# A fused graph-and-convolution layer on one core: when the convolution's sums are evacuated, when position factors are made, and in which order a batch's graph pieces are issued

## The chip, the core and the metric

The kernel runs on one core of a Trainium2 chip. The metric is the device time of one execution in microseconds (us), and smaller is better. In the profile TensorE is called PE (its weight loads PEld), VectorE DVE, ScalarE ACT, GpSimd POOL; SP is the engine whose queue issues all DMAs here.

## The reference

The layer takes x, 32 batches of 512 rows with 256 columns, and a 512x512 adjacency mask for each batch, all in float32. With h the normalised and rectified x:

```python
h = jnp.maximum(_layernorm(x, axis=-1), 0.0)
x = x + _L0_gnn_ref(h, adj, ...)

# inside _L0_gnn_ref (its x is h above, d = 256)
xc = jnp.transpose(x, (0, 2, 1))
h = relu(_bn(_conv1d(xc, conv1_w, 0), ...))          # width 1
h = _bn(_conv1d(h, conv2_w, 8), ...)                 # width 17
x_conv = jnp.transpose(relu(h + xc), (0, 2, 1))
s = x @ w_se.T + b_se                                # 3 position values a row
sq = jnp.sum(s * s, axis=-1)
dist = sq[:, :, None] + sq[:, None, :] - 2.0 * jnp.einsum('bnd,bmd->bnm', s, s)
A = jnp.exp(-dist) * mask
msg = relu(x @ w_msg.T + b_msg)
x_nmp = jnp.einsum('bnm,bmd->bnd', A, msg)
x_in = jnp.concatenate([x_conv, x_nmp], axis=-1)
gi, gh = x_in @ w_ih.T + b_ih, x @ w_hh.T + b_hh
r = sigmoid(gi_r + gh_r); z = sigmoid(gi_z + gh_z)
nn_ = jnp.tanh(gi_n + r * gh_n)
return (1.0 - z) * nn_ + z * x
```

## The kernel before

**Two streams of work.** The 32 batches are taken in 8 rounds of G = 4. The convolution of width 17 is computed by a nested fast scheme: from the rows of a round, VectorE forms 25 operand sets (`operands`, `fives`: five first-level operands `x1`, and five `x2` from each), 25 transformed weight sets `w` are loaded again for each round, and 25 products of matmuls go to the PSUM tile `ps_c` (3 buffers). `convolution` issues each product in two halves. `summed(g)` takes the 25 products, in five groups of five, and adds them into the tile `y`: a product is copied or added out of PSUM at once (`n`, `z`, `s`), while the later additions are put into the list `SUMS` and issued one by one by `sum_some`, at every second half of a product. At the second product of a group whatever still stands in `SUMS` is issued. When a round's 25 products are done, the rest of `SUMS` is issued at once, and then eight ScalarE evacuations (L393, two for each of the four batches) write `y` with scale and shift into the four `xconv` tiles.

The other stream is `others(g)`. In round g it runs `rest` for the four batches of the round before, and, ahead of the fourth, `rows(g+1)`: the transposes and the width-1 convolution for the next round. The normalisation of those rows (`norm`) is cut into pieces of DVE and POOL work that `norm_some` issues, one with each step of the others, once `rows_begin` has loaded x; that is at the third batch (n == 2).

**The order.** Nothing is planned at run time: each engine's instructions run in the order in which this program issues them. `step_conv` and `step_other` advance the two streams, and the variable `ahead` holds their balance: each step of the others says its TensorE time in us (the number that it yields), which is multiplied by a share (81/214 in most rounds) and paid for by half products of 1.65. Behind the last round the four last batches run without any convolution.

**One batch, `rest(b, following)`.** In order: load of the mask and of the hidden rows `hTb` if they are not loaded yet; `positions(b)` (one PE piece, two DVE instructions that write rows of `left` and `right`, two ACT squares that write others: L462 to L465); the residual addition of the convolution and its relu (L527, L528); `messages` twice (PE, then DVE and ACT); `kernel_exp` for four columns of the 512x512 kernel matrix (L480 matmul of `left` and `right`, L481 exponential); `finish` of the batch before in two pieces (L500 transposes of its result `o_sb`, L504 addition, store); `masked` for four columns (L488 transposes of the mask, L489 multiplication into `at`). That is called the graph part here. Then the loads for the following batch are issued, and the gates follow: for each half o the hidden part of the candidate, at o = 0 the two `gather` matmul groups, the reset gate r, the update gate z, the candidate n, and on POOL the last three operations, which write `o_sb`. PSUM tiles: `ps_acc` has 3 buffers (messages, exponentials, gathers, gates), `ps_tr` has 2 (positions, masks, finishes, row transposes).

Of the kernel before, what the change touches and what calls it, by code (L numbers as in the profile page):

```python
# [29 lines left out]
G = 4  # L30
U = 57
# [9 lines left out]
def kernel(  # L41
# [293 lines left out]
    def sum_some(pieces=1):  # L335
        while SUMS and pieces:
            SUMS.pop(0)()
            pieces -= 1

    def summed(g):  # L340


        y = cv.tile([P, 3, 3, NZ], F32, name="y")
        yf = y.rearrange("p f e n -> p f (e n)")

        def add(dst, a, b, op=ALU.add):
            SUMS.append(lambda: nc.vector.tensor_tensor(dst, a, b, op=op))  # L347

        def copy(dst, src, scale):
            SUMS.append(lambda: nc.scalar.activation(dst, src, AF.Copy, scale=scale))  # L350

        def twice(dst, a, b):
            SUMS.append(
                lambda: nc.vector.scalar_tensor_tensor(dst, a, 2.0, b, op0=ALU.mult, op1=ALU.add)
            )

        for j1 in ORDER:
            ps = yield
            n3 = cv.tile([P, NZ], F32, name="n", bufs=3)
            nc.scalar.activation(n3, ps, AF.Copy)  # L360
            ps = yield
            sum_some(len(SUMS))
            z = y[:, 0] if j1 == 3 else cv.tile([P, 3, NZ], F32, name="z")
            ends = z[:, 0:3:2, :]
            zf = z.rearrange("p e n -> p (e n)")
            nc.vector.tensor_tensor(z[:, 0, :], ps, n3, op=ALU.add)  # L366
            ps = yield
            nc.vector.scalar_tensor_tensor(z[:, 2, :], n3, 4.0, ps, op0=ALU.mult, op1=ALU.add)
            ps = yield
            n2 = cv.tile([P, NZ], F32, name="n", bufs=3)  # L370
            nc.scalar.activation(n2, ps, AF.Copy)
            ps = yield
            s = cv.tile([P, NZ], F32, name="s")
            nc.vector.tensor_tensor(s, ps, n2, op=ALU.add)
            nc.vector.tensor_tensor(n2, ps, n2, op=ALU.subtract)
            add(ends, ends, s[:, None, :].to_broadcast([P, 2, NZ]))
            twice(z[:, 1, :], n3, n2)
            if j1 == 3:
                copy(yf[:, 1], zf, 2.0)
                copy(yf[:, 2], zf, 4.0)  # L380
            elif j1 in (0, 4):
                add(yf[:, j1 // 2], yf[:, j1 // 2], zf)
            else:
                for e in range(3):
                    add(yf[:, e], yf[:, e], zf, ALU.subtract if (e, j1) == (1, 2) else ALU.add)
        sum_some(len(SUMS))
        if late is None:
            late_pools()
        for b in range(g * G, (g + 1) * G):
            xc = XC[b] = late.tile([P, ND, 9 * U], F32, name="xconv", bufs=4)  # L390
            for o in range(ND):
                c = o * NU + b % G * U
                nc.scalar.activation(  # L393
                    xc[:, o, :].rearrange("p (u e f) -> p f e u", e=3, f=3), y[:, :, :, c : c + U],
                    AF.Identity, bias=bn2_sh[:, o : o + 1], scale=bn2_sc[:, o : o + 1],
                )
        yield

    AHEAD, AHEAD_W = 4, 2
    XC = {}  # L400

    def convolution():

# [110 lines left out]
    def rest(b, following):  # L514

        if b not in MS:
            load_adj(b)
        if b not in HB:
            load_h(b)
        msg = late.tile([P, NT, D], F32, name="msg")  # L520
        at = late.tile([P, NT, N], F32, name="at")
        xnmp = late.tile([P, ND, N], F32, name="xnmp")
        positions(b)
        yield 1.75
        xc = XC.pop(b)
        xconv = xc[:, :, :N]
        nc.vector.tensor_tensor(xconv, xconv, HB[b], op=ALU.add)  # L527
        nc.scalar.activation(xconv, xconv, AF.Relu)  # L528
        for c in range(0, NT, 2):
            messages(b, msg, c)  # L530
            yield 1.8
        for c in range(NT):
            kernel_exp(at, c)
            yield 0.87
        while waiting:
            for c in range(0, NT, 2):
                finish(*waiting[0], c)
                yield 0.55
            waiting.pop(0)
        for c in range(NT):  # L540
            masked(b, at, c)
            yield 0.55
        MS.pop(b)
        if following is not None:
            load_adj(following)
            load_h(following)
        hT = HB.pop(b)
        o_sb = late.tile([P, ND, N], F32, name="o_sb")
        x_in = [xconv[:, i, :] for i in range(ND)] + [xnmp[:, i, :] for i in range(ND)]

        def cols(o, g):
            return slice(g * D + o * P, g * D + (o + 1) * P)

        def hidden(o, g):
            return [(whh[:, i, cols(o, g)], hT[:, i, :]) for i in range(ND)]

        def given(o, g):
            return [(wih[:, i, cols(o, g)], x_in[i]) for i in range(2 * ND)]

        for o in range(ND):  # L560
            ps_h = acc.tile([P, N], F32, name="ps_acc")
# [15 lines left out]
            yield 5.2  # L577
            ps_z = acc.tile([P, N], F32, name="ps_acc")
            matmul_sum(ps_z, hidden(o, 1) + given(o, 1))
            z = late.tile([P, N], F32, name="z")  # L580
            nc.scalar.activation(z, ps_z, AF.Sigmoid, bias=brz[:, ND + o : ND + o + 1])  # L581
            yield 5.2
            ps_n = acc.tile([P, N], F32, name="ps_acc")
            matmul_sum(ps_n, given(o, 2))
            nc.vector.tensor_tensor(r, ps_n, r, op=ALU.add)  # L585
            nc.scalar.activation(  # L586
                r, r, AF.Tanh,
                bias=vec[:, _COL["b_ih"] + 2 * ND + o : _COL["b_ih"] + 2 * ND + o + 1],
            )

            t = late.tile([P, N], F32, name="gate_t")
            nc.gpsimd.tensor_tensor(t, hT[:, o, :], r, op=ALU.subtract)  # L592
            nc.gpsimd.tensor_tensor(t, z, t, op=ALU.mult)
            nc.gpsimd.tensor_tensor(o_sb[:, o, :], r, t, op=ALU.add)
            if o == ND - 1:
                load_res(b)
            yield 3.46
        waiting.append((b, o_sb))

    def rows_begin(g):  # L600
# [34 lines left out]
    def others(g):  # L635


        bs = list(range((g - 1) * G, g * G)) if g > 0 else []
        for n, b in enumerate(bs[:-1]):
            if n == 2 and g + 1 < NG:  # L640
                rows_begin(g + 1)
            yield from rest(b, b + 1)
        if not bs:
            rows_begin(g + 1)
        yield "rows wanted", g + 1
        if g + 1 < NG:
            yield from rows(g + 1)
        yield "rows made", g + 1
        for b in bs[-1:]:
            yield from rest(b, b + 1)  # L650
# [3 lines left out]
    for g in range(NG):  # L654
        other = others(g)
        share = 81.0 / (214.0 if 0 < g < NG - 1 else 196.0 if g else 18.0)
        ahead = 0.0
        end = ended = False
        blocked = False

        def step_other():

            nonlocal ahead, end, made
            if end:
                return False
            norm_some()
            got = next(other, None)
            if got is None:
                end = True
                return False  # L670
            if isinstance(got, tuple):
                if got[0] == "rows wanted":
                    while freed < g:
                        step_conv()
                else:
                    made = got[1]
                return True
            ahead += got * share
            return True
# [78 lines left out]
```

## Time and profile before

| | |
|---|---|
| time, median of 3 runs | 2671.2 us (2666.92 to 2671.62) |
| the profiled execution | 2667.14 us |
| its span, first to last instruction | 2665.4 us |
| mean granted TensorE clock | 0.949 of full speed |
| PE busy | 2441.9 us |
| DVE busy | 1228.8 us |
| ACT busy | 640.5 us |
| POOL busy | 328.6 us |
| DMA | 231.15 MB, 87 GB/s on average |

All durations in this document's rows come from that profiled execution. A row of instructions reads: start, duration, engine, line of the kernel, operation, output <- inputs, shape, count, and in brackets the idle time of the engine just before with what ended it. A row of waits reads: engine, tile and line that waited, what it waited for, us in total, times, longest. A matmul in float32 is counted twice (two passes each).

### The profile page before, as it was taken

The page shows a single profiled execution, that of the slowest core. Times are in us where ns is not written, and L with a number is a line of the kernel's source. Part 1 is how long each engine was busy: PE and PEld are TensorE (multiplying, and loading weights), DVE is VectorE, ACT ScalarE, POOL GpSimd, SP SyncE. Part 2 cuts the span into 40 slices and gives each one's busy share as a digit, 9 for nine tenths or more (in the row PEclk, how much of TensorE's full clock was granted, in tenths as well). Part 3 has the DMA queues.
Part 4 walks back from the last instruction along what each step waited for, and adds up shares of the span by engine and source line. Part 5 has one row for each costly group of instructions (what it writes and reads, how often), then busy time and mean ns, then how long its engine had stood idle before and what let it go on. Part 6 is the DMA issues. An engine that isn't in the chain of part 4 may idle for free.

```text
span 2665.4 us, 20881 instructions
## 1 busy us (share of the span) xinstructions
PE 2441.9 (92%) x8192; PEld 1505.2 (56%) x8192; DVE 1228.8 (46%) x1766; ACT 640.5 (24%) x882; POOL 328.6 (12%) x240
## 2 busy tenths in 40 slices
PE   6689999899997999979999799997999979997998
PEld 4566556465564565645556465664556646664444
DVE  7983364534545344444444445344454444443222
ACT  3232213212133121222212222222212132212222
POOL 1000121110101111011110011100111101111111
PEclk9789999999998999989999899998999989998999
DMA  5242223123231232322232122221232212220110
GB/s 214 100 170 72 79 95 127 47 79 103 79 119 47 71 111 81 117 71 65 92 105 102 55 87 101 97 79 63 87 103 93 82 64 86 87 95 25 54 40 24
DMA packets 108996, 231.15 MB, mean 87 GB/s; under 512 B 8418, under 2 KB 57698, under 8 KB 108258
## 3 DMA queue, kind: packets, MB, share of 16 engines
q1 hardware_dynamic: 108898, 229.82, 25.1%
q8 instruction: 64, 1.05, 0.2%
q14 instruction: 34, 0.28, 0.0%
HBM read 183.13 MB, written 46.66 MB: 86 GB/s over the span
## 4 chain that ended last, share of the span: by engine, by line
PE 80%; DVE 12%; ACT 4%; issue 2%; DMA 1%; POOL 1%; SPq 0%; POOLq 0%; DVEq 0%; ACTq 0%
PE ps_acc L86 51%; PE ps_c L86 20%; PE ps_acc L480 4%; ACT xconv L393 2%; PE ps_tr L488 2%; DVE x L239 2%; PE ps_tr L86 2%; DVE y L347 1%; PE ps_tr L217 1%; DVE x L242 1%; PE ps_tr L500 1%; DVE at L489 1%; DVE st L182 1%; DVE y L504 1%; DVE z L347 1%
## 5 line engine op out<-in xcount | busy, mean ns | idle before, releaser
L86 PEld LDWEIGHTS ps_c<-x,w 128*128 128x128 f32 x3200 | 619.8, 195 | 180.0 <-issue 153.0
L86 PE MATMUL ps_c<-x,w 128*128 128x228 f32 x3200 | 694.1, 364 | 22.7 <-DVE z L366 10.7
L86 PE MATMUL ps_acc<-hTb,whh 128*128 128x512 f32 x768 | 365.1, 601 | 0.0
L86 PE MATMUL ps_acc<-xconv,wih 128*128 128x512 f32 x768 | 360.8, 592 | 0.0
L86 PE MATMUL ps_acc<-xnmp,wih 128*128 128x512 f32 x768 | 360.6, 592 | 0.0
L592 POOL TENSOR_TENSOR gate_t<-hTb,r 128x512 f32<-128x512 f32 x64 | 91.1, 1423 | 2020.3 <-issue 1272.9
L480 PE MATMUL ps_acc<-right,left 67*128 67x512 f32 x256 | 155.3, 739 | 120.8 <-ACT left L465 99.2
L573 DVE SCALAR_TENSOR_TENSOR r<-ps_acc,vec,r 128x512 f32<-128x512 f32 x64 | 48.1, 751 | 441.9 <-ACT r L571 441.9
L86 PEld LDWEIGHTS ps_acc<-xnmp,wih 128*128 128x128 f32 x768 | 145.3, 189 | 184.2 <-issue 184.2
L86 PEld LDWEIGHTS ps_acc<-xconv,wih 128*128 128x128 f32 x768 | 145.8, 190 | 157.3 <-issue 156.9
L86 PE MATMUL ps_acc<-at,msg 128*128 128x512 f32 x512 | 228.5, 592 | 0.0
L585 DVE TENSOR_TENSOR r<-ps_acc,r 128x512 f32<-128x512 f32 x64 | 44.3, 692 | 396.8 <-PE ps_acc L86 396.8
L86 PEld LDWEIGHTS ps_acc<-hTb,whh 128*128 128x128 f32 x768 | 146.0, 194 | 117.0 <-issue 116.1
L571 ACT ACT_TABLE_LOAD x32 | 41.1, 1283 | 652.1 <-PE ps_acc L86 652.1
L242 DVE SCALAR_TENSOR_TENSOR x<-x,x 128x471 f32<-128x471 f32 (+1 forms) x184 | 159.4, 866 | 5.2
L480 PEld LDWEIGHTS ps_acc<-right,left 67*128 67x128 f32 x256 | 54.5, 225 | 185.6 <-ACT left L465 102.5
L239 DVE TENSOR_TENSOR x<-x 128x471 f32<-128x471 f32 x200 | 158.0, 808 | 1.4
L86 PEld LDWEIGHTS ps_acc<-at,msg 128*128 128x128 f32 x512 | 97.2, 190 | 106.4 <-issue 106.2
L494 DVE COPY xnmp<-ps_acc 128x512 f32<-128x512 f32 x64 | 44.3, 692 | 236.4 <-PE ps_acc L86 236.4
L581 ACT ACTIVATE z<-ps_acc,brz 128x512 f32<-128x512 f32 x64 | 44.0, 688 | 341.2 <-PE ps_acc L86 341.2
L586 ACT ACTIVATE r<-r,vec 128x512 f32<-128x512 f32 x64 | 46.2, 722 | 307.5 <-DVE r L585 307.5
L86 PE MATMUL ps_acc<-hT,w 128*128 128x512 f32 x256 | 119.1, 607 | 0.0
(90 smaller groups left out, 2242.0 us busy)
## 6 DMA issues: line engine op xcount, KB each, us to landing
w<-wd SPq DMA_DIRECT2D x175, 512.0 KB, 3.3
m_sb<-in_adj_dram SPq DMA_DIRECT2D x32, 1024.0 KB, 5.3
x_sb<-in_x_dram SPq DMA_DIRECT2D x32, 512.0 KB, 6.2
hd<-hT SPq DMA_DIRECT2D x32, 512.0 KB, 2.9
hTb<-hd SPq DMA_DIRECT2D x32, 512.0 KB, 6.2
y<-in_x_dram SPq DMA_DIRECT2D x64, 256.0 KB, 4.0
out_dram<-y SPq DMA_DIRECT2D x64, 256.0 KB, 2.2
wd<-w SPq DMA_DIRECT2D x25, 512.0 KB, 2.6
```

The lines of the kernel that those rows point to most:

```text
L86: nc.tensor.matmul(ps, lhsT, rhs, start=(i == 0), stop=(i == len(pairs) - 1))
L239: nc.vector.tensor_tensor(dst, get(a), get(b), op=ALU.subtract)
L242: nc.vector.scalar_tensor_tensor(dst, a, -2.0, b, op0=ALU.mult, op1=ALU.add)
L347: SUMS.append(lambda: nc.vector.tensor_tensor(dst, a, b, op=op))
L393: nc.scalar.activation(xc[:, o, :].rearrange("p (u e f) -> p f e u", e=3, f=3), y[:, :, :, c : c + U], AF.Identity, bias=bn2_sh[:, o : o + ...
L480: nc.tensor.matmul(ps, left[:, c * P : (c + 1) * P], right, start=True, stop=True)
L488: nc.tensor.transpose(ps[:, n * P : (n + 1) * P], m[:, n, c * P : (c + 1) * P], ident)
L494: nc.vector.tensor_copy(xnmp[:, d, :], ps)
L573: nc.vector.scalar_tensor_tensor(r, ps_h, vec[:, _COL["b_hh"] + 2 * ND + o : _COL["b_hh"] + 2 * ND + o + 1], r, op0=ALU.add, op1=ALU.mult,)
L585: nc.vector.tensor_tensor(r, ps_n, r, op=ALU.add)
L586: nc.scalar.activation(r, r, AF.Tanh, bias=vec[:, _COL["b_ih"] + 2 * ND + o : _COL["b_ih"] + 2 * ND + o + 1],)
L592: nc.gpsimd.tensor_tensor(t, hT[:, o, :], r, op=ALU.subtract)
```

## The change

Five things are moved; the arithmetic stays.

1. The eight evacuations are no longer issued at the round's end. Each is an entry of `SUMS`, behind the last additions, so that it is issued during the next round's first steps. `step_other` now issues one entry of `SUMS` at each step while more than four are left. The tile `y` is taken only when the next round first writes it. A batch that needs its `xconv` issues entries until its own evacuations are out.
2. `positions` of the following batch is called between the two halves of the gates. Only a batch whose mask was not loaded ahead (the first) still calls it at its start.
3. The graph part alternates: messages ahead of columns 0 and 2, and for each column the exponential and at once its mask; behind columns 1 and 3 one piece of `finish`.
4. The residual addition and relu move behind the graph part.
5. `rows_begin` is called at the first batch of a round (n == 0) instead of the third, and, except in round 0, `norm_some` at every second step only.

```diff
     def summed(g):
-        y = cv.tile([P, 3, 3, NZ], F32, name="y")
-        yf = y.rearrange("p f e n -> p f (e n)")
+        y = yf = None
...
             ps = yield
             sum_some(len(SUMS))
+            if y is None:
+                y = cv.tile([P, 3, 3, NZ], F32, name="y")
+                yf = y.rearrange("p f e n -> p f (e n)")
             z = y[:, 0] if j1 == 3 else cv.tile([P, 3, NZ], F32, name="z")
...
-        sum_some(len(SUMS))
         if late is None:
             late_pools()
         for b in range(g * G, (g + 1) * G):
-            xc = XC[b] = late.tile([P, ND, 9 * U], F32, name="xconv", bufs=4)
             for o in range(ND):
-                c = o * NU + b % G * U
-                nc.scalar.activation(xc[...], y[:, :, :, c : c + U], AF.Identity, ...)
+                SUMS.append(lambda b=b, o=o: evacuate(y, b, o))
         yield
+    def evacuate(y, b, o):
+        if o == 0:
+            XC[b] = late.tile([P, ND, 9 * U], F32, name="xconv", bufs=4)
+        c = o * NU + b % G * U
+        nc.scalar.activation(XC[b][...], y[:, :, :, c : c + U], AF.Identity, ...)
+        if o == ND - 1:
+            evacuated.add(b)
...
     def rest(b, following):
         if b not in MS:
             load_adj(b)
-        if b not in HB:
             load_h(b)
+            positions(b)
+            yield 1.75
         msg, at, xnmp = ...
-        positions(b)
-        yield 1.75
-        xc = XC.pop(b)
-        xconv = xc[:, :, :N]
-        nc.vector.tensor_tensor(xconv, xconv, HB[b], op=ALU.add)
-        nc.scalar.activation(xconv, xconv, AF.Relu)
-        for c in range(0, NT, 2):
-            messages(b, msg, c)
-            yield 1.8
         for c in range(NT):
+            if c % 2 == 0:
+                messages(b, msg, c)
+                yield 1.8
             kernel_exp(at, c)
             yield 0.87
-        while waiting:
-            for c in range(0, NT, 2):
-                finish(*waiting[0], c)
-                yield 0.55
-            waiting.pop(0)
-        for c in range(NT):
             masked(b, at, c)
             yield 0.55
+            if waiting and c % 2:
+                finish(*waiting[0], c - 1)
+                yield 0.55
+        waiting.clear()
         MS.pop(b)
         if following is not None:
             load_adj(following)
             load_h(following)
         hT = HB.pop(b)
+        while b not in evacuated:
+            sum_some()
+        xc = XC.pop(b)
+        xconv = xc[:, :, :N]
+        nc.vector.tensor_tensor(xconv, xconv, hT, op=ALU.add)
+        nc.scalar.activation(xconv, xconv, AF.Relu)
...
             yield 3.46
+            if o == 0 and following is not None:
+                positions(following)
+                yield 1.75
         waiting.append((b, o_sb))
...
     def others(g):
-            if n == 2 and g + 1 < NG:
+            if n == 0 and g + 1 < NG:
                 rows_begin(g + 1)
...
         def step_other():
-            norm_some()
+            steps += 1
+            if g == 0 or steps % 2:
+                norm_some()
+            if len(SUMS) > 4:
+                sum_some()
             got = next(other, None)
```

More of the change, by code (lines that the diff above doesn't have):

```diff
@@ L389, in summed @@
         for b in range(g * G, (g + 1) * G):
-            xc = XC[b] = late.tile([P, ND, 9 * U], F32, name="xconv", bufs=4)
             for o in range(ND):
-                c = o * NU + b % G * U
[L393 to L396, printed above, removed]
-        yield
+                SUMS.append(lambda b=b, o=o: evacuate(y, b, o))
+        yield
+    def evacuate(y, b, o):
+        if o == 0:
+            XC[b] = late.tile([P, ND, 9 * U], F32, name="xconv", bufs=4)
+        c = o * NU + b % G * U
+        nc.scalar.activation(
+            XC[b][:, o, :].rearrange("p (u e f) -> p f e u", e=3, f=3), y[:, :, :, c : c + U],
+            AF.Identity, bias=bn2_sh[:, o : o + 1], scale=bn2_sc[:, o : o + 1],
+        )
+        if o == ND - 1:
+            evacuated.add(b)
     AHEAD, AHEAD_W = 4, 2
-    XC = {}
+    XC, evacuated = {}, set()
     def convolution():
@@ L657 @@
         ahead = 0.0
+        steps = 0
         end = ended = False
@@ L661, in step_other @@
         def step_other():
-            nonlocal ahead, end, made
+            nonlocal ahead, end, made, steps
             if end:
                 return False
-            norm_some()
+            steps += 1
[3 more added lines that the diff above has]
+                sum_some()
             got = next(other, None)
```

## The prediction

> **What bounds the kernel now.** I read the page's first lines, then who TensorE waits for, then the granted clock in short stretches, then the order of instructions where the waits are.
>
> ```profile
> span 2665.4 us, 20881 instructions
> PE 2441.9 (92%) x8192; PEld 1505.2 (56%) x8192; DVE 1228.8 (46%) x1766; ACT 640.5 (24%) x882; POOL 328.6 (12%) x240
> ```
>
> TensorE (PE) is busy 92% of the span; VectorE (DVE) and ScalarE (ACT) are not half busy. So only two things can move the time: the 224 us in which PE idles, and stretches in which PE is busy but slow. The waits of PE alone:
>
> ```profile
> PE ps_acc L480 <- ACT left L465: 99.2, 9, 16.0
> ...
> PE ps_tr L488 <- DVE y L504: 17.9, 19, 1.8
> PE ps_acc L480 <- ACT at L481: 15.8, 15, 1.4
> ```
>
> The first row is 44% of the idle time in nine waits. By windows of one round it is one wait of 13.0 us at the start of each of rounds 2 to 7, one of 16.0 us behind the last round, and 5 us elsewhere. The clock by windows of PE (columns: stretch, length, PE busy, granted clock as a share of full speed, DMA): first the start of one round, then three graph parts of that round (its batches 1, 2 and 3), then the whole round.
>
> ```profile
> 1478.00:1518.00 40.00, 26.63 (x90) 0.74 0.13 42
> 1487.00:1499.70 12.70, 0.00 (x0) 0.65 0.14 41
> 1499.70:1510.00 10.30, 10.29 (x18) 0.50 0.00 0
> ...
> 1570.00:1590.00 20.00, 17.88 (x71) 0.91 0.25 83
> 1645.00:1662.00 17.00, 12.68 (x45) 0.80 0.18 55
> 1738.00:1754.00 16.00, 15.58 (x75) 1.00 0.22 69
> ...
> 1493.00:1817.00 324.00, 303.80 (x1024) 0.95 0.25 86
> ```
>
> The round's start loses twice: 13.4 us of idle PE, and then 10.3 us at clock 0.50, which is 5.2 us of lost work: 18.6 us. Batch 1 loses 2.1 idle and at most (1-0.91)x20 = 1.8 of clock; batch 2, with the normalisation's pieces on DVE, 4.3 and at most 3.4; batch 3 only 0.4. The Trainium skill (TensorE: Matmul & The Clock Gate, "What's actually happening") says that PE falls to half rate after an idle window of about 3.4 us and is back after a busy one as long. The fall agrees (0.65 over 12.7 us is half clock from some 4 us into the wait); the return doesn't: 0.50 holds for over 10 us. By the Trainium skill's figure the slow stretch would cost an estimated 1.7 us, not 5.2.
>
> Why the start waits, in order of time (start, duration, engine, line, operation, out<-in, count):
>
> ```profile
> 1478.25 1.88 PE L86 MATMUL ps_tr<-hTb,wse 128*67 128x512 f32 x4
> 1478.45 0.69 DVE L585 TENSOR_TENSOR r<-ps_acc,r 128x512 f32<-128x512 f32 x1 [8.03 <-PE ps_acc L86]
> 1480.27 2.01 DVE L347 TENSOR_TENSOR z<-z,s 128x912 f32<-128x912 f32 x1
> 1482.20 1.69 DVE L354 SCALAR_TENSOR_TENSOR z<-n 128x456 f32<-128x456 f32 x1
> 1483.92 5.52 DVE L347 TENSOR_TENSOR y<-y,z 128x1368 f32<-128x1368 f32 x3
> 1489.48 8.79 ACT L393 ACTIVATE xconv<-y,bn_shift,bn_scale 128x513 f32<-128x513 f32 x8 [9.58 <-DVE y L347]
> 1493.02 1.28 DVE L475 TENSOR_TENSOR msg<-ps_acc,bmsg 128x512 f32<-128x512 f32 x2
> 1494.21 2.08 DVE L239 TENSOR_TENSOR x<-h 128x1415 f32<-128x1415 f32 x1
> 1496.33 1.63 DVE L242 SCALAR_TENSOR_TENSOR x<-x,x 128x1415 f32<-128x1415 f32 x1
> 1498.00 0.79 DVE L239 TENSOR_TENSOR x<-x 128x471 f32<-128x471 f32 x1
> 1498.97 0.68 ACT L465 ACTIVATE left<-ps_tr,bse 3x512 f32<-3x512 f32 x1
> 1499.71 7.20 PE L480 MATMUL ps_acc<-right,left 67*128 67x512 f32 x8 [13.04 <-ACT left L465]
> 1512.35 2.96 DVE L489 TENSOR_TENSOR at<-ps_tr,at 128x512 f32<-128x512 f32 x4
> 1516.07 1.70 PE L86 MATMUL ps_c<-x,w 128*128 128x228 f32 x8
> 1517.61 7.03 PE L86 MATMUL ps_acc<-at,msg 128*128 128x512 f32 x16
> ```
>
> The positions' matmuls are done at 1480. Their factors stand on DVE behind the last sums (until 1489.4) and on ACT behind all eight evacuations (8.79 us, 1.1 each), so the exponential's matmul (L480) starts at 1499.7.
>
> **The change, part by part.** Counts stay: 64 evacuations, 32 positions, the same table loads and DMAs. Only places move.
>
> *Positions one batch ahead.* Two DVE and two ACT instructions of 0.7 us and one PE piece (1.72 us, from 1478.25 to the next start) go between the two halves of the gates, where PE runs without a wait; cost 0. It needs the next batch's hidden rows by then: that load is issued where it was, ahead of the gates. If it came late PE would wait; the only such wait today is the first batch's, which stays in line as it is.
>
> *Evacuations and last sums spread.* One of 13 pieces is now issued with each step of the others and each half product. I worked out the order: last-round tail, z add, z twice, messages 0, half product, y add three times with column 0 and 1 and two statistics pieces between them, evacuations among the columns, finish 0, messages 2, columns 2 and 3. Prices of what PE does there, at full clock, from batch 3 of this round, and of the normalisation's pieces:
>
> ```profile
> 1739.04 3.62 PE L86 MATMUL ps_acc<-wmsg,hTb 128*128 128x256 f32 x16
> ...
> 1744.90 2.74 PE L480 MATMUL ps_acc<-right,left 67*128 67x512 f32 x6
> ...
> 1749.89 1.03 PE L488 MATMUL ps_tr<-ident,m_sb 128*128 128x128 f32 x8
> ...
> L182 DVE BATCH_NORM_STATS2 st<-x_sb 128x6 f32<-128x256 f32 x128 | 51.7, 404 | 18.8 <-DMA x_sb<-in_x_dram 18.8
> L190 DVE TENSOR_SCALAR x_sb<-x_sb,mv,rstd 128x256 f32<-128x256 f32 x128 | 45.2, 408 | 26.2 <-POOL rstd L143 26.2
> L183 DVE BATCH_NORM_AGGREGATE mv<-st 128x2 f32<-128x6 f32 x128 | 23.3, 182 | 4.4
> ```
>
> From the end of the old batch's last gate (time 0, 1478.25 above), DVE in its new order: 0.2 + 1.8 (three ops, 1478.45 to 1480.27) + 1.9 + 1.7 (z) + 0.6 (message) + 0.8 (operand) + 5.5 (y) + one statistics piece 2x(0.40+0.18) = 1.2 + 0.7 (mask of column 0) = 14.4. PE gets there sooner: messages 1.8, half products 2x1.6, two exponentials 2x0.9, two masks 2x0.5: 7.8. Then *finish 0* wants one of the two ps_tr buffers and waits for column 0's multiply: 6.6 us. That is what is late next, and it is long enough to take the clock to 0.50. From 14.4: finish 1.0 and messages 3.6 at half clock (19.0), add 0.7, relu 0.6, exponential 0.6 plus its matmul (21.6), multiply (22.3); then DVE holds a first-level operand, 2.08+1.63+0.79 = 4.5, and a scaling piece 0.8 in front of column 3's multiply: 28.3. The gathering matmul starts there. Today it starts 1517.61-1478.25 = 39.4 after time 0, which includes 1.72 of positions and one half product (1.54) that now comes behind it, so 36.1 of like work. **Gain 7.8 a round start; six of them, 47 us.** Ends: DVE alone (25 us of work up to column 3, less some 2 us that the two z ops lose while POOL runs) could let it start at 23 to 24, a gain of 12; every link waiting for the next could bring 34, a gain of 2. I take the worked value, nearer the rows. The y tile's first write of the new round now waits for the last evacuations; three ps_c buffers cover it.
>
> *Rows begun at batch 0, every other step.* The normalisation leaves batch 2 (loss 7.7) and goes half to the round's start (counted above), half to batch 1 (loss 3.9). I take 3 each for both afterwards: (7.7-3)+(3.9-3) = 5.6 for each of the six rounds that have such rows, **33 us**; ends 0 and 9. Its three x loads go to SP's queue at the round's start: 512 KB each behind weight loads that wait for buffers, and DMA share there is 0.13, so 0; if late, DVE waits with statistics, not the weights.
>
> *Behind the last round.* No convolution is left, so sums are issued only after the graph part. Rows (the old round's last batch, then the batch after):
>
> ```profile
> 2426.82 1.88 PE L86 MATMUL ps_tr<-hTb,wse 128*67 128x512 f32 x4
> ...
> 2469.09 1.88 PE L86 MATMUL ps_acc<-hTb,whh 128*128 128x512 f32 x4
> ...
> 2498.27 1.88 PE L86 MATMUL ps_tr<-hTb,wse 128*67 128x512 f32 x4
> ...
> 2503.94 1.27 POOL L594 TENSOR_TENSOR o_sb<-r,gate_t 128x512 f32<-128x512 f32 x1
> ...
> 2513.12 1.88 PE L86 MATMUL ps_acc<-hTb,whh 128*128 128x512 f32 x4
> ```
>
> Today 42.3 us from positions to the reset gate. Afterwards: graph part 12.5 and finish's add 0.8; then DVE: z twice and y adds 0.9+5.5, two evacuations 2.5 on ACT, residual add 1.2, and behind it the copy of the first gather, whose buffer the reset gate needs: 24.1, where PE is ready at about 21. With the positions' 1.72: 25.8. **Gain 16 us**; ends 10 and 20.
>
> *Alternation in the tail.* A batch's graph part takes 2513.12-2498.27 = 14.9 (13.1 without positions) there. New: finish 0 comes 4.5 us after the gates, but POOL writes o_sb until 6.9: PE waits 2.4, and the mask of column 2 waits for its exponential; some 12.5 to 13.5. Taken as 0 to 0.4 worse for three batches: **-1 us**.
>
> The start of the first round keeps its 9.9 us wait for the first load: 0, at most 5 won. **Sum:** 47+33+16-1 = 95 at the worked values; since the half clock behind the new 6.6 us wait will last past the gather's start in some rounds (10 us is what it lasts above), I take off 1 us for each of six: 89. The profiled execution took 2667.1 us (span 2665.4), 4 below the median of 2671.2: 2667-89 = **2578**, which is 93 below the median.
>
> **The rivals.**
>
> *The waits vanish.* If POOL doesn't slow DVE and no wait reaches the length that halves the clock, a start gains 12, both graph parts all but lose their loss (9 a round), the tail 20: 6x12+6x9+18 = 144; with half of the second, 2667-130 = **2537**. For it: batch 3 above, with little else on DVE, runs at clock 1.00. Against: 25 us of DVE work in front of a multiply that PE wants much earlier. The Trainium skill (TensorE: Matmul & The Clock Gate, "Part 4: PE-mode transpose") says transposes do not count as PE work for the clock; alternated with real matmuls they would leave fewer such windows. Rows agree in part: at 0.80 stands the part with the most stalled transposes, but batch 3 has as many at 1.00.
>
> *The wait only changes its name.* Column multiplies queue behind sums and statistics, ACT's exponentials behind evacuations; the start's gather comes at 34, a gain of 2, and batch 1 loses what batch 2 wins (half of 33): 12+16+15 = 43: **2624**. For it: DVE order is strict in the trace, and the change puts 2 to 3 us of statistics where DVE is fullest. Against: the left factors leave the chain altogether, and ACT's 8.8 us block is broken up.
>
> *Slower.* Alternating chains PE exponential, ACT, DVE multiply and the next transpose. If the buffers did not let columns overlap, a column costs 0.9+0.6+0.7 and the hand-overs 0.6 = 2.8, four of them 11, messages 3.5 and finish 1: 15.7 against the tail's 13.1, and batch 1's 1.8 of clock on top: +4.4 for 32 batches = 141, against the 89: **2719**. It decides from 2.8 a batch on. Against: three ps_acc and two ps_tr buffers, and half products between the steps.
>
> **How the numbers follow.** Forecast (2555 to 2600) 0.58; waits vanish 0.20; name changed 0.17; slower 0.05. 2578 is the forecast's. The range 2530 to 2622 takes in the first rival's value and nearly the second's, and leaves out some 0.2; the likeliest case's own is 2555 to 2600. About 0.2% (5 us) is what a measurement of this kernel can tell from no change. Faster 0.93 (the first three cases, less a little), same 0.02, slower 0.05.
>
> **What would show it.** Right: no wait of L480 for left but the first batch's; at each round's start a PE wait of 4 to 8 us before finish (L500) for DVE's multiply, some 31 us from the last gate to the gather by like counting; batch 2's window at clock above 0.9; the time from the last round's end to the reset gate 16 us shorter; POOL named before L500 in the tail. Wrong: waits of L488 and L500 for DVE that sum to over 80 us; clock 0.50 in every graph part; DVE waiting for x loads at the round's start; the gates' positions waiting for hTb.

## The result, and the profile after

The changed kernel takes 2542.9 us (median of 4 runs, 2541.4 to 2544.9). Before, in the same comparison, it is 2669.3 us. The ratio is 0.953, with a 95% interval of 0.951 to 0.954. The profiled execution took 2544.2 us (before 2667.1), so 123 us are to be found between the two traces; the prediction's sum found 89 of them. One execution of all those told of here stands apart: the last experiment's kernel took 6954.8 us once, in the execution that was profiled, and 2488.8 to 2492.6 us in its other four, so nothing is read from its trace.

The first lines of the page after, and the waits of PE alone:

```profile
span 2542.4 us, 20857 instructions
PE 2386.9 (94%) x8192; PEld 1484.4 (58%) x8192; DVE 1224.5 (48%) x1766; ACT 646.4 (25%) x882; POOL 335.2 (13%) x240
```

```profile
PE ps_tr L508 <- DVE at L497: 70.1, 23, 6.2
...
PE ps_tr L86 <- DMA hTb<-hd: 15.5, 1, 15.5
```

The 99.2 us for `left` are gone. In their place stands the wait that the prediction named: finish (L508 now) for the multiplies of the mask (L497), 70.1 us. PE's busy time fell as well, by 55 us for the same 8192 matmuls. The clock explains most of that: laid over the stretches of half clock in the two traces, PE was busy at half speed for 174 us before and 89 us after, which is some 43 us less lost to it, about a third of the 123 us. The other 12 us of the fall I have not placed. Windows of PE as before: the start of a round (time zero, the end of the old batch's last gate, is at 1421.64), its wait, the 4.6 us behind the wait, then the graph parts of batches 1, 2 and 3.

```profile
1418.00:1458.00 40.00, 33.76 (x123) 0.91 0.28 92
1429.00:1435.40 6.40, 0.21 (x2) 0.79 0.00 0
1435.40:1440.00 4.60, 4.54 (x13) 0.55 0.32 81
1497.00:1517.00 20.00, 16.99 (x74) 0.91 0.12 41
1569.00:1586.00 17.00, 16.34 (x76) 1.00 0.17 57
1661.00:1677.00 16.00, 15.97 (x78) 1.00 0.14 49
```

Rows of that start in order of time:

```profile
1421.64 1.89 PE L86 MATMUL ps_acc<-wmsg,hTb 128*128 128x256 f32 x8
...
1423.65 1.10 DVE L346 TENSOR_TENSOR z<-z,s 128x912 f32<-128x912 f32 x1
1423.72 2.16 POOL L599 TENSOR_TENSOR gate_t<-hTb,r 128x512 f32<-128x512 f32 x1 [19.29 <-ACT r L593]
...
1428.04 4.12 DVE L346 TENSOR_TENSOR y<-y,z 128x1368 f32<-128x1368 f32 x2
1428.95 0.60 ACT L489 ACTIVATE at<-ps_acc 128x512 f32<-128x512 f32 x1
...
1433.16 1.55 DVE L346 TENSOR_TENSOR y<-y,z 128x1368 f32<-128x1368 f32 x1
1434.62 0.68 DVE L497 TENSOR_TENSOR at<-ps_tr,at 128x512 f32<-128x512 f32 x1
...
1435.46 1.08 PE L508 MATMUL ps_tr<-ident,o_sb 128*128 128x128 f32 x4 [6.25 <-DVE at L497]
...
1436.34 3.49 PE L86 MATMUL ps_acc<-wmsg,hTb 128*128 128x256 f32 x8
...
1439.67 1.02 PE L488 MATMUL ps_acc<-right,left 67*128 67x512 f32 x2
...
1441.74 0.69 DVE L497 TENSOR_TENSOR at<-ps_tr,at 128x512 f32<-128x512 f32 x1 [0.54 <-ACT at L489]
...
1445.96 3.60 PE L86 MATMUL ps_acc<-at,msg 128*128 128x512 f32 x8
...
1447.55 0.69 DVE L497 TENSOR_TENSOR at<-ps_tr,at 128x512 f32<-128x512 f32 x1
```

Finish waits 6.25 us for column 0's multiply and starts 13.8 us after time zero. Column 0's exponential was done at 1429.55; its multiply stands on DVE behind three y additions, with statistics between them. Half clock follows (messages take 3.49 instead of 1.89), but the next exponential's matmuls are at full speed (1.02), and gathering starts at 24.3.

To place all of the 123 us I measured every batch's graph part in both traces as the time from its first message matmul to its first gather matmul (the first four rows of the table). These parts do not hold quite the same half products in both kernels: summed over the rounds, the starts hold 19 after and 18 before, batch 2 holds 15 and 20, batch 3 holds 21 and 16, batch 1 the same 21. A half product takes 1.54 us at full clock, and the column "won, like work" takes out each half product at that price. Sums over the rounds, in us:

| part | before | after | won | won, like work | predicted |
|---|---|---|---|---|---|
| starts of rounds 2 to 7 (6) | 215.3 | 148.3 | 67.0 | 68.5 | 41 |
| batch 1 (7) | 142.8 | 142.0 | 0.8 | 0.8 | in the 33 below |
| batch 2 (7) | 161.6 | 108.7 | 52.9 | 45.2 | 33 with batch 1 |
| batch 3 (7) | 110.6 | 113.4 | -2.8 | 4.9 | 0 |
| up to the first message matmul | 201.0 | 205.4 | -4.4 | -4.4 | 0 |
| from batch 28's first message to the end | 236.8 | 222.2 | 14.6 | 14.6 | 15 |
| gates of all rounds, and the first batch's part | | | -5.1 | -6.6 | 0 |

### The profile page after: what moved, and what is told of

Its sections match the earlier page's. It is cut to its first block, busy times and chain, and to the rows that moved or that the text cites. A ratio compares the mean times of both kernels' runs of the same rounds, so it can differ in the third digit from the quotient of the medians.

```text
span 2542.4 us, 20857 instructions
## 1 busy us (share of the span) xinstructions
PE 2386.9 (94%) x8192; PEld 1484.4 (58%) x8192; DVE 1224.5 (48%) x1766; ACT 646.4 (25%) x882; POOL 335.2 (13%) x240
## 4 chain that ended last, share of the span: by engine, by line
PE 83%; DVE 13%; ACT 1%; issue 1%; DMA 1%; POOL 0%; SPq 0%; POOLq 0%; DVEq 0%
PE ps_acc L86 55%; PE ps_c L86 20%; PE ps_acc L488 3%; PE ps_tr L86 2%; DVE x L239 2%; DVE x L242 2%; DVE y L346 2%; PE ps_tr L508 2%; PE ps_tr L496 1%; PE ps_tr L217 1%; DVE at L497 1%; DVE msg L483 1%; DVE z L346 1%; DVE z L353 0%; DVE st L182 0%
## 5 line engine op out<-in xcount | busy, mean ns | idle before, releaser
L86 PEld LDWEIGHTS ps_c<-x,w 128*128 128x128 f32 x3200 | 612.6, 193 | 172.3 <-issue 142.7
L86 PE MATMUL ps_c<-x,w 128*128 128x228 f32 x3200 | 685.1, 360 | 23.7 <-DVE z L368 10.5
L242 DVE SCALAR_TENSOR_TENSOR x<-x,x 128x471 f32<-128x471 f32 (+1 forms) x184 | 165.1, 897 | 5.1
L86 PE MATMUL ps_acc<-wmsg,hTb 128*128 128x256 f32 x512 | 137.5, 417 | 0.0
L488 PE MATMUL ps_acc<-right,left 67*128 67x512 f32 x256 | 133.9, 604 | 0.0
L497 DVE TENSOR_TENSOR at<-ps_tr,at 128x512 f32<-128x512 f32 x128 | 86.5, 687 | 87.5 <-ACT at L489 83.9
```

The source lines that it names most:

```text
L86: nc.tensor.matmul(ps, lhsT, rhs, start=(i == 0), stop=(i == len(pairs) - 1))
L242: nc.vector.scalar_tensor_tensor(dst, a, -2.0, b, op0=ALU.mult, op1=ALU.add)
L488: nc.tensor.matmul(ps, left[:, c * P : (c + 1) * P], right, start=True, stop=True)
L497: nc.vector.tensor_tensor(at[:, c, :], ps, at[:, c, :], op=ALU.mult)
```

## The experiments

Each was timed against the kernel before in the same session (before: 2665.8 to 2666.2 us there). "Parts" are measured as in the table above; for the whole change they are 148 (starts), 142, 109 and 113 (batches 1, 2, 3). Where a kernel holds other half products in a part than the one it is compared with, that is said.

**Factors in line again.** From the changed kernel:

```diff
         if b not in MS:
             load_adj(b)
             load_h(b)
-            positions(b)
-            yield 1.75
+        positions(b)
+        yield 1.75
...
-            if o == 0 and following is not None:
-                positions(following)
-                yield 1.75
```

> The changed kernel, but each batch makes its own position factors at its start again. Theory (the spread evacuations carry the gain at the round starts; the factors alone cost little once nothing stands in front of them): the two DVE and two ACT instructions come out about 7 us after the last gate, PE stands about 3.4 us before the first exponential, and the wait before finish shrinks by part of it: 1 to 3 us at each of seven starts, up to 1 us for the other batches; 2543 becomes 2555 to 2570. Rival (the factors ahead of time are what freed the starts): at least half of the 67 us that the starts won goes back, 2577 or more.

Measured: 2580.4 us, ratio 0.968 (0.966 to 0.969), 38 us slower than the change. That is more than the theory's range and just over the rival's bound, so by its time the rival stands. By parts it doesn't: the half products of this kernel are spread as in the kernel before, and counted as like work the starts lose 20.3, 30% of their gain and not half, batch 2 loses 12.0, batch 1 4.4 and batch 3 3.5. So the factors do not carry the starts, but in line they cost over 3 us at each, just above the most that I had put. Of batch 2's 12.0, 9.5 fall in the first round alone. There the factors stand on DVE behind first-level operands, PE waits for `left`, and the clock halves:

```profile
342.84 5.18 DVE L239 TENSOR_TENSOR x<-h 128x1415 f32<-128x1415 f32 x2
...
355.23 2.08 PE L488 MATMUL ps_acc<-right,left 67*128 67x512 f32 x2 [6.52 <-ACT left L473]
```

The waits of PE over the whole run:

```profile
PE ps_tr L508 <- DVE at L497: 45.6, 19, 4.3
PE ps_acc L488 <- ACT left L473: 42.1, 17, 6.5
```

Here 42 us of waiting for `left` come back and only 25 us of the other wait go away.

**Evacuations at once again.** From the changed kernel:

```diff
+        sum_some(len(SUMS))
         if late is None:
             late_pools()
         for b in range(g * G, (g + 1) * G):
             for o in range(ND):
-                SUMS.append(lambda b=b, o=o: evacuate(y, b, o))
+                evacuate(y, b, o)
```

> The changed kernel, but the last sums and all eight evacuations are issued in one block at the round's end again; the factors stay one batch ahead. Theory: ACT's block of 8.8 us stands in front of the relu and the exponentials, so column 0's multiply comes some 9 us later and PE waits some 15 us before finish instead of 6; the starts lose 9 to 11 us each, the last one some 8: 2543 becomes 2605 to 2620. Rival (the factors ahead of time carry the starts): up to 2555.

The edit issues the last additions at once as well, as the kernel before did. Measured: 2607.6 us, ratio 0.978 (0.976 to 0.979), 65 us slower than the change, in the theory's range. The starts take 205.6, so 57 of their 67 us go back, and batch 28's part, behind the last round, grows from 17.8 to 33.0. One start:

```profile
1457.06 8.70 ACT L401 ACTIVATE xconv<-y,bn_shift,bn_scale 128x513 f32<-128x513 f32 x8 [9.74 <-DVE y L346]
1468.12 0.69 DVE L498 TENSOR_TENSOR at<-ps_tr,at 128x512 f32<-128x512 f32 x1 [8.72 <-ACT at L490]
...
1468.96 1.09 PE L509 MATMUL ps_tr<-ident,o_sb 128*128 128x128 f32 x4 [15.72 <-DVE at L498]
```

The block of eight stands in front of the exponentials on ACT; DVE waits 8.7 us for column 0's exponential, and PE 15.7 for DVE. The block is worth nearly three times what the factors are at the starts (57 us against 20).

**Rows at the third batch again.** From the changed kernel:

```diff
-            if n == 0 and g + 1 < NG:
+            if n == 2 and g + 1 < NG:
...
-            if g == 0 or steps % 2:
-                norm_some()
+            norm_some()
```

> The changed kernel, but the next round's rows begin at the third batch, one piece with each step, as before. Theory (the loss in batch 2's graph part came from the normalisation on DVE, and moving it is what won 52 us there): batch 2's part grows by 5 to 8 us in six rounds, while round starts and batch 1 win 2 to 4 us together; 2543 becomes 2550 to 2580. Rival (the alternated order cured batch 2, the rows' place doesn't matter): within 5 us of 2543 or below, since the starts then have less DVE work.

Measured: 2555.6 us, ratio 0.958 (0.957 to 0.960), 13 us slower. Batch 2 takes 137.8 (29 more), the starts 139.7 (8.6 less), with the same half products in each. So moving the normalisation and halving its pace explains 29 of the 45 us that batch 2 won as like work, some 5 in each round; factors ahead of time are another 12 by the first experiment. It also shows what the move costs elsewhere. SP's queue at the start of the first round, first with the rows moved back, then after the change:

```profile
181.34 0.38 SPq L97 DMA_DIRECT2D m_sb<-in_adj_dram  x1
181.76 1.21 SPq L101 DMA_DIRECT2D hTb<-hd  x1
```

```profile
182.13 6.45 SPq L93 DMA_DIRECT2D x_sb<-in_x_dram  x3
188.69 1.06 SPq L97 DMA_DIRECT2D m_sb<-in_adj_dram  x1
189.80 1.95 SPq L101 DMA_DIRECT2D hTb<-hd  x1
```

The three x loads hold the queue for 6.5 us ahead of the first batch's own loads, and PE's wait for `hTb` is 15.5 us instead of 11.2. That happens once: half of all x loads take 0.5 us or less on that queue, and PE waits for `hTb` in no later round.

**The graph part in its old order.** From the changed kernel, the loop of messages, exponentials, finishes and masks as it stood before.

```diff
-        for c in range(NT):
-            if c % 2 == 0:
-                messages(b, msg, c)
-                yield 1.8
-            kernel_exp(at, c)
...
+        for c in range(0, NT, 2):
+            messages(b, msg, c)
+            yield 1.8
+        for c in range(NT):
+            kernel_exp(at, c)
+            yield 0.87
...
```

> The changed kernel, but the graph part in its old order: messages, exponentials, finishes, masks. Theory (alternation is worth little by itself; it puts finish behind column 0's multiply, which is the wait of 6 us at each start): starts between 2 us better and 2 us worse, batches 1 and 2 within 1 us, tail 0.5 us a batch worse: 2530 to 2560. Rival (alternation cured batch 2's part by keeping the transposes apart): 30 us or more worse, 2573 or more.

Measured: 2557.2 us, ratio 0.959 (0.957 to 0.960), 14 us slower. Batch 2 takes 109.8, as with the alternation: that did not cure it, and the rival falls. The time is in the theory's range, but not by its parts: the starts lose 17.1, nearly 3 us each where at most 2 were expected, batch 3 loses 5.3, and batch 1 wins 8.2. So the alternation is worth something at the starts and in batch 3 and costs in batch 1. My reading is that it helps where DVE and ACT are the late ones and costs where finish is put behind a late multiply; no run here isolates that.

**One large part alone, on the kernel before.** First the factors ahead of time, then the spread evacuations (with the residual addition behind the graph part):

```diff
 # factors alone: rest() of the kernel before
-        positions(b)
-        yield 1.75
...
+            if o == 0 and following is not None:
+                positions(following)
+                yield 1.75
```

> The kernel before with one part of the change alone: each batch's position factors are made between the halves of the gates of the batch before. Theory (at a round start the evacuations' block on ACT also stands in front of relu and exponentials, so freeing the factors alone only moves the wait): starts win 1 to 3 us each, the other batches 0.5 to 1 each; 2666 becomes 2640 to 2655. Rival (the factors' wait of 13 us is the loss, and is gone): starts win 10 us or more each, 2600 or less.

```diff
 # evacuations alone: summed(), step_other() and rest() of the kernel before
+                SUMS.append(lambda b=b, o=o: evacuate(y, b, o))
...
+            if len(SUMS) > 4:
+                sum_some()
...
+        while b not in evacuated:
+            sum_some()
```

> The kernel before with the other large part alone: last sums and evacuations spread over the next round's pieces, and the residual addition behind the graph part, which that needs; factors, order and rows as before. Theory (the block is the loss; parts nearly add up, as 65+38+13+14 from the undone parts against 125 for the whole says): starts win 6 to 8 us each, the last 14; 2666 becomes 2598 to 2618. Rival (with the factors in line the exponentials wait for DVE's sums instead): less than 35 won, 2631 or more.

Measured: the factors alone 2648.8, ratio 0.994 (0.992 to 0.995), 17 us won; the evacuations alone 2573.5, ratio 0.966 (0.964 to 0.967), 92 us won, better than the 48 to 68 expected. The time with the factors alone is in the theory's range, but not by its way: the starts don't win 1 to 3 us each, they grow by 12 as like work (from 215 to 229 as they stand), while batches 1 and 2 win 29 together. The starts' wait has only changed its name:

```profile
PE ps_acc L480 <- DVE msg L475: 64.2, 9, 11.0
PE ps_acc L480 <- ACT at L481: 34.0, 10, 4.5
```

With the evacuations alone the starts are 162.4, 53 of the 67, and the tail's first part falls from 33.7 to 14.9. Both orders of taking the change apart agree on the larger part (65 undone, 92 alone) and on the smaller (38, 17). But the evacuations are worth more alone than on top of the rest, and the factors less; why the two do not add was not traced.

**Normalisation later; sums held.** Two edits that are in neither kernel, to test that DVE's queue sets the start's new wait. The second comes on top of the first:

```diff
-            if g == 0 or steps % 2:
+            if g == 0 or (steps > 12 and steps % 2):
                 norm_some()
```

> The changed kernel, but the normalisation's pieces begin only behind the first 12 steps of a round, so not in the start's graph part. Theory (DVE's queue sets the start's length; e3's starts were 1.4 us shorter each without these pieces, and its loss was all in batch 2): starts 1 to 2 us shorter, batch 1 unchanged as it has as many pieces as before; 2543 becomes 2530 to 2538. Rival (what the pieces leave is filled by another wait, ACT's): 2540 to 2546.

```diff
-            if len(SUMS) > 4:
+            if len(SUMS) > 4 and steps > 12:
                 sum_some()
```

> As the kernel with the normalisation later, and the others' steps issue no sums or evacuations during the first 12 steps of a round (half products still issue one each); they come from the end of the start's graph part on, as behind the last round. Theory (PE waits before finish because column 0's multiply stands behind the y additions on DVE): the wait of 6 us goes, the start's part falls from 24.7 us towards the 16.1 that batch 3 takes, the additions are covered by the gathers; 6 to 8 us at six starts: 2543 becomes 2490 to 2508. Rival (the additions delay the residual and the gather's copies instead, as 4 us behind the last round): 2515 to 2535.

Normalisation later alone: 2537.4 us, ratio 0.952 (0.950 to 0.954), which does not stand apart from the change's 0.953. The time lies in the theory's range and the starts win 6.8, 1.1 each as it said, but batch 1, which it left unchanged, loses 4.3; this run alone decides nothing. With the sums held too: 2507.2 us, ratio 0.940 (0.939 to 0.942), 1.3% below the change by the two ratios, some 33 us. The starts fall to 100.7, 16.6 each, as expected, and the finish pieces wait 39.8 us in all instead of 70.1:

```profile
PE ps_tr L508 <- DVE at L497: 39.8, 22, 4.1
```

The multiplies of columns 0 and 1 at one start now stand ahead of the y additions:

```profile
1409.25 1.27 DVE L497 TENSOR_TENSOR at<-ps_tr,at 128x512 f32<-128x512 f32 x2
1410.44 1.57 DVE L346 TENSOR_TENSOR y<-y,z 128x1368 f32<-128x1368 f32 x1
```

They begin 6.4 us after that start's first message matmul (1402.86), where column 0's began 13.0 us after it in the changed kernel, and PE's wait before finish falls from 5.1 to 6.2 us at the six starts to 0.6 us or less. So the start's wait was the y additions in front of a multiply, and to a smaller part the statistics; the evacuations, which this edit holds back too, run on ACT, where column 0's exponential was not late. Some of the gain is given back in batch 1 (154.5 against 142.0), where the normalisation now stands whole.

**Batch 1's wait.** On the kernel with the sums held, first the normalisation only in the gates, then also both finish pieces behind the fourth mask:

```diff
-            if g == 0 or (steps > 12 and steps % 2):
+            if g == 0 or GATES:          # filled behind the graph part, emptied behind the gates
                 norm_some()
```

> As the kernel with the sums held, but the normalisation's pieces are issued only with the gates' steps of a batch, one a step, none in a graph part. Theory (batch 1's wait of 3.4 us before finish stands behind a first-level operand, 5 us, and one statistics piece, 1.2; it is just long enough to halve the clock): the wait falls to some 2.2 us, the slow stretch goes, batch 1's part from 22.2 to 17 to 20: 2507 becomes 2480 to 2497. Rival (the operand alone keeps the wait and the half clock): 2500 or more.

```diff
             masked(b, at, c)
             yield 0.55
-            if waiting and c % 2:
-                finish(*waiting[0], c - 1)
-                yield 0.55
+        for c in range(0, NT, 2):
+            if waiting:
+                finish(*waiting[0], c)
+                yield 0.55
```

> As the kernel with the normalisation in the gates, but the two finish pieces come behind the fourth mask, so PE has messages 2, exponential 2 and half products to do before a third transpose piece wants column 0's multiply. Theory: some 3 us more cover, no wait before finish in batch 1, the tail's wait for POOL gone: 0.5 to 3 us a batch part, 2470 to 2492. Rival (the same wait stands before the third mask instead): within 4 us of the kernel it is built on.

The first: 2501.8 us, ratio 0.938 (0.937 to 0.940), not clearly apart from 0.940, and batch 1's part is 154.0 as it was: the expected time was missed and the rival's number came. But the edit did not take the normalisation off the wait. In each of rounds 2 to 6 the two statistics pieces are gone from there, and two scaling pieces, issued with the last gates, run on DVE at the beginning of the graph part instead; column 0's multiply starts 8.6 us after the first message matmul in both kernels. One round (first message matmul at 1469.53):

```profile
1469.81 2.73 DVE L190 TENSOR_SCALAR x_sb<-x_sb,mv,rstd 128x256 f32<-128x256 f32 x2
...
1473.06 2.64 DVE L239 TENSOR_TENSOR x<-h 128x1415 f32<-128x1415 f32 x1
...
1478.10 1.28 DVE L497 TENSOR_TENSOR at<-ps_tr,at 128x512 f32<-128x512 f32 x2
1478.93 1.09 PE L508 MATMUL ps_tr<-ident,o_sb 128*128 128x128 f32 x4 [3.37 <-DVE at L497]
```

So whether the first-level operand of 5 us alone keeps the wait is open. The second: 2488.3 us, ratio 0.933 (0.932 to 0.935), the best kernel here, 2.0% below the change by the two ratios. Batch 1 wins 31 (123.0), its wait before finish falling from 3.4 to 0.6 us, and the tail's parts some 9, both more than expected; not expected was that the starts lose 26 (126.8), because there the second finish piece now waits for column 3's multiply behind the first-level operand:

```profile
1408.46 1.63 DVE L242 SCALAR_TENSOR_TENSOR x<-x,x 128x1415 f32<-128x1415 f32 x1
1410.13 0.78 DVE L239 TENSOR_TENSOR x<-x 128x471 f32<-128x471 f32 x1
1410.83 0.69 DVE L497 TENSOR_TENSOR at<-ps_tr,at 128x512 f32<-128x512 f32 x1
...
1411.57 0.66 PE L508 MATMUL ps_tr<-ident,o_sb 128*128 128x128 f32 x4 [3.20 <-DVE at L497]
```

Finish between the columns at a start and behind them elsewhere was not run.

**Does the exponentials' matmul hold the clock down?** After its wait the kernel before ran for over 10 us at half clock, the changed one for 4.6. The first work behind the wait differs: exponential matmuls over 67 rows before, transposes and messages over 128 after. On the kernel before:

```diff
-    left = const.tile([67, N], F32)
-    right = const.tile([67, N], F32)
+    left = const.tile([P, N], F32)
+    right = const.tile([P, N], F32)
```

> The kernel before, with the two operands of the exponentials' matmul laid out over 128 rows (the added rows are zero); nothing else moved. Theory (matmuls over 67 rows do not count as enough work for the clock, so after the 13 us wait it returns only with the products behind the eight exponential matmuls): the slow stretch after each start's wait, 11 us, shrinks by some 5 to 7, worth 2.5 to 3.5 us at seven starts: 2666 becomes 2640 to 2650. Rival (the clock's return depends on the length of the wait alone): 2661 to 2668.

> The kernel with finish behind the masks, with the exponentials' operands over 128 rows. Theory (rows count for the clock, but few slow stretches are left): 0 to 8 us below that kernel. Rival (rows do not count): within 3 us of it.

Measured: 2645.0 us, ratio 0.992 (0.991 to 0.994): 21 us won by rows of zeros, in the theory's range; the six starts win 18.0 of them and the last one 2.4. The wait is the same 13.04 us. The half product behind the eight exponential matmuls in the kernel before, and the matmuls and that product with full rows:

```profile
1506.69 3.25 PE L86 MATMUL ps_c<-x,w 128*128 128x228 f32 x8
```

```profile
1491.51 5.95 PE L480 MATMUL ps_acc<-right,left 128*128 128x512 f32 x8 [13.04 <-ACT left L465]
1497.30 1.70 PE L86 MATMUL ps_c<-x,w 128*128 128x228 f32 x8
```

The eight matmuls take 5.95 instead of 7.20 us, and the product behind them 1.70 instead of 3.25: the clock is back within six. On the best kernel, where few slow stretches are left, the same edit gives 2490.6 us over its four like executions, ratio 0.934 (0.933 to 0.936): no change clear of noise. The rival allowed that; the theory's 0 to 8 us below were not seen.

## Why the prediction was right, and by how much it missed

The direction, the range and the mechanism of the largest term were right. The value, 2578, was 35 us high, and the measured time lies outside the likeliest case's own 2555 to 2600; several terms missed, some in opposite directions.

- *The starts.* Right: the wait of finish on column 0's multiply (6.6 predicted, 6.25 measured; at 14.4 and 13.8 from time zero), finish and messages at half clock behind it (4.6 and 4.4), and that the block of evacuations is the larger cause (undone: 57 of 67 us back). Mis-sized: the start of the gather, 28.3 predicted and 24.3 measured. I let it wait for column 3's multiply; it runs column by column, started at 1445.96 and reached its last pair of matmuls only after that multiply had ended (1448.24). That is 2.3 us. The other 1.7 are that the multiply itself ended at 26.6: finish started 0.6 sooner, and column 2's multiply ended 2.6 us behind the messages, where I had added 3.3. I then took off another 1 us a round for a slow stretch past the gather, but the clock was back after 4.6 us. Together 67 instead of 41.
- *Rows begun earlier.* I left a loss of 3 us in batch 2; the window shows 0.7 us of idle time and clock 1.00. As like work batch 2 won 45: the rows' move is 29 of it and factors ahead of time 12, which stood in no term. Batch 1, put at 3, kept 3.0 of idle and up to 1.8 of clock: nothing won there. What the move adds at the starts (8.6) I had counted there.
- *Three x loads at cost 0.* Wrong. They hold SP's queue for 6.5 us in front of the first batch's hidden rows, whose wait grew from 9.9 to 15.5 us. I had named the weight loads as what is queued with them and overlooked the first batch's own loads behind them.
- *Behind the last round.* 15 predicted and 14.6 measured is luck: two misses cancel. To the reset gate I predicted 16, and it is 13.8 by like counting (26.8 us from the first message matmul, and 1.7 of positions, against 42.3 before). The graph part there takes 16.1 us up to the candidate's hidden part (2336.22), where I had put 12.5: finish waits 3.6 us for DVE, and the messages behind it run at half clock (3.62 us). Behind the wait for the first gather's copy, which I did have, the gate runs at half clock. Against that, the three graph parts that follow won 2.6 us, where I had put a loss of 1: finish waits 1.6 us there, not 2.4, and for DVE, not for POOL. The rows behind the last round:

```profile
2320.15 1.89 PE L86 MATMUL ps_acc<-wmsg,hTb 128*128 128x256 f32 x8
...
2328.22 1.08 PE L508 MATMUL ps_tr<-ident,o_sb 128*128 128x128 f32 x4 [3.58 <-DVE at L497]
...
2346.93 3.23 PE L86 MATMUL ps_acc<-hTb,whh 128*128 128x512 f32 x4 [1.95 <-DVE xnmp L502]
```

- *Batch 3 and the gates.* Both stood at 0. As like work batch 3 won 4.9, and the alternation explains it (undone: 5.3 back). The gates lost 4.4 us behind the first round's first gathers, a wait of 2.0 us and half clock, and 3.1 us in batch 2's, for which I have no cause.
- *The rivals.* The waits did not vanish (70 us of them are left), so the first rival's mechanism is not what happened, though the time is only 6 us from its 2537. That value does not follow from its own terms either: with half of the graph parts' 54 the sum is 117, not 130, and the time 2550. Batch 2 did reach clock 1.00 as it said; the starts and batch 1 did not. The wait changed its name with the factors alone, as the second rival has it, and not with the whole change. The slower rival's serial chain appears in no part.
- *The clock.* The Trainium skill (TensorE: Matmul & The Clock Gate, "What's actually happening") says that the clock is back after a busy window of some 3.4 us. I set it aside because the trace before held half clock for over 10 us. Behind full-row work the runs are near it (4.6 us here, within 5.95 with full rows); behind 67-row matmuls they are not.

## What to carry to other kernels

When a wait is named, list all that stands between the waiting instruction and its releaser on that engine's queue: here one ACT instruction was named, and a block of eight in front of it was the larger cause; freeing the factors alone put 98 us of other waits in the place of the 99. Parts compared between two kernels should hold the same work: one half product more in a round turned batch 3's gain into a loss. Work that is spread should be spread to where the engine that takes it has cover: putting sums and normalisation behind the start's graph part won another 1.3% over putting them between its pieces. And a wait costs more than its length when the clock falls, so what follows it matters too.

## What was not expected of the hardware

A matmul over 67 of the 128 rows is as long as a full one at full clock (two passes 1.02 us both ways: at 1439.67 in the changed kernel, and with zeros filled in below), but eight of them did not bring TensorE's clock back from half speed; with the missing rows filled with zeros the clock was back within 6 us, and the kernel before became 21 us faster with the same instructions. Which number of rows is enough was not measured. The full-row one, where the clock is back:

```profile
1730.89 1.02 PE L480 MATMUL ps_acc<-right,left 128*128 128x512 f32 x2
```
